# A graph layer with a mixture of low-rank experts on one core: two steps' operations in a new order, the gathers in two runs, the gate's sum on ScalarE

## The chip, the core and the metric

The kernel runs on one core of a Trainium2 chip. Its time is device time in microseconds (us). Of the kernel before there are three runs: 1904.98, 1907.07 and 1908.52 us; their median, 1907.07, is the time that the prediction starts from. The names of the engines in the rows are: PE for TensorE's matmuls, PEld for its weight loads, DVE for VectorE, ACT for ScalarE, POOL for GpSimd, SP for SyncE, which issues most DMAs.

## The reference

There are 128 graphs of 128 nodes, with 1024 features each, in float32. The matrix `adj` holds counts between nodes (about 3% of the entries are set).

```python
x = x + elu(gat(layernorm(x), adj))      # one layer of graph attention
x = x + moe(layernorm(x))                # a mixture of low-rank experts

def gat(h, adj):                         # 16 heads of 64 features
    Wh = (h @ W) split into heads
    e = leaky_relu(Wh . a1 + Wh . a2)    # per node of a row, per head
    att = softmax(where(adj == 0, -9e15, e)) * adj
    return att @ Wh, heads side by side

def moe(y):                              # 8 experts of rank 16, 2 of them chosen
    gates = softmax over the top two of y[row 0 of the graph] @ router_w.T
    return sum_e gates[e] * ((y @ lora_down[e].T) @ lora_up[e].T)
```

The experts of a graph are chosen by its first row alone, and all of its 128 rows then use them.

## The kernel before

**Tiles and steps.** Graphs are taken in pairs (64 pairs, q = 0 to 63) and in groups of four (32 groups, g). Step q multiplies pair q by W, does the attention, the two layer norms and the residual sums of pair q-1, and one half of the experts' work for the group that the pairs before form: odd and even steps together make a group, so everything repeats every two steps. Steps 0 and 1, and those after the last pair, are ordered by another function (`at_the_ends`).

**The product by W** is Strassen's with seven products of half blocks, `M1` to `M7`, each in two halves (`M1a`, `M1b`): eight passes on TensorE for one half (L529), accumulated in a bank of PSUM. Reading a bank is done on VectorE (`u2`, `u4`, `c22`, `c21`, `c12`: L536) or ScalarE (`p1`: L541); `f` adds a part on GpSimd (`add_other`, L553). M3 of two pairs is done jointly by an inner product of seven parts, `I1` to `I7` (L593), which is read by `ip`, `ipa`, `r` and `s` (L599 to L611). The pair sums `ps0` to `ps3` (L462) and inner sums `is0` to `is3` (L472) make the products' inputs on GpSimd. The result's high and low parts come from `hi` (ScalarE, L664) and `lo` (VectorE, L668).

**The attention** of graph t of a pair: `A` (four matmuls, L723), `h` (L729), `x` (L736), `e` (ScalarE, L739), `y` (L746), then the second layer norm's mean on GpSimd (`n`, L751), its squares on ScalarE (`q`, L755) and, on GpSimd, the small `ss` (L776 to L783) and part of the inner product, `ipa` (L602). `t` copies a graph's halves on ScalarE (L796) and transposes them by a DMA; `rj` (L802) and `jn` (L823) put them together again. `st` and `rs` are the first layer norm's statistics and rstd (L401 to L406).

**The experts' work** of a group: `ro`, `sr`, `rp` (L852 to L858) and `L` (a router matmul, L891) give eight logits a graph; `ch0` and `ch1` choose the top two; `ra` takes one exponential on ScalarE (L938); `wg` makes the gates on VectorE (L944 to L946); `fr` computes the rows to fetch (L955, L958); `fe` gathers them by nine indirect DMAs on GpSimd's queue (eight at L968 for the down matrices, one at L972 for the up matrices); `D` is the down matmul (L982, 64 small matmuls), `dn` its gate on ScalarE (L993), `U0` and `U1` the up matmuls for the two halves of the features (L1002, eight instructions in two pairs of banks, one bank for each graph), and `v00`, `v01`, `v10`, `v11` add two graphs' banks each to the residual on VectorE (L1011). `v10` and `v11` also issue the output's stores on SP's queue (L1014). Each double bank has two buffers, which `pd`, `pu`, the attention's `ph` and the inner products share: U1's first pair of banks must have been read by v00, its second by v01.

**Loads.** `lx` loads the next pair (L152), `lt` its transpose x_t (L157), `lc` the counts of three groups ahead (L161), `la` the counts transposed (L166). `ac` (L479 `nz`, L482 `n`) and `an` (L488 to L493) prepare the mask of a group two ahead from the counts.

**What sets the order.** Nothing is reordered by a scheduler. A step from 2 to 63 runs the names of one of two lists, `EVEN` or `ODD`, one after the other, and issues each operation at once. A name with a minus sign belongs to the step before. So the lists alone are the order of every engine's queue and of every DMA queue:

```python
for name in (EVEN, ODD)[q % 2]:
    if q > 2 or not name.endswith("-"):
        do(q, name)
```

Of the kernel before, what the change touches and what calls it, by code (L numbers as in the profile page):

```python
# [8 lines left out]
F32 = mybir.dt.float32  # L9
# [4 lines left out]
AF = mybir.ActivationFunctionType  # L14
ALU = mybir.AluOpType
# [6 lines left out]
TINY = 1e-30  # L22

EVEN = """
lo0- e1- M5b- wg- M5a- M7a- y1- ac- M7b- u4- c22- ps0- ro1- c12- n0- q0- t0- D- M4b- t1-
st0- n1- ps1- dn- st1- q1- an- U0- M1b v00- ss- v01- rj0- M4a- U1- c21- ro0- v10- aw hi3-
hi1- M1a ps3- v11- rs- hi2- lo1- lo3- M6a lc- rj1- jn0- lo2- p1 A0 jn1- lt pe ps2- M6b A1 u2
""".split()

ODD = """  # L30
aw2- M2b- M2a- M5b- h0- hi0- ps0- ps1- x0- sc0- ps3- lx- h1- M5a- lo0- is0- M7a- x1- e0- y0-
e1- u4- is2- ro0- M7b- y1- n0- c22- q0- is1- ro1- sr- is3- st0- n1- I7- I6- t0- ps2- I1- ip-
q1- M4a- ipa- st1- r- ss- I5- rp- I4- s- M4b- c21- rs- L- hi2- I3- ch0- d1- lo2- hi3- I2-
ch1- t1- fr- M6a d0- aw rj0- M1b M1a hi1- la- pe lo1- aw2 lo3- M6b A0 jn0- h0 lx p1 jn1- u2
A1 x0 rj1- fe- h1 M2b x1 lt e0 M2a f hi0 sc0 ra- y0
""".split()


# [2 lines left out]
def adj_ffn_kernel(  # L41
# [16 lines left out]
    nc = tc.nc  # L58
    B, N, D = x.shape
    P = 128  # L60
    KC = D // P
# [5 lines left out]
    R = ER // E  # L67
    TOP = 2
# [5 lines left out]
    NG, _, G, _ = adj.shape  # L74
# [8 lines left out]
    work = ctx.enter_context(tc.tile_pool(name="work", bufs=2))  # L83
# [12 lines left out]
    GRP = {}  # L96
# [831 lines left out]
    def own(val, name):  # L928

        mine = small.tile([P, G * TOP], F32, tag="own", name="own", bufs=2)  # L930
        nc.vector.tensor_tensor(mine, val.rearrange("p g s -> p (g s)"), slot, ALU.mult)
        got = small.tile([P, 1], F32, tag=name, name=name)
        nc.vector.tensor_reduce(got, mine, AX.X, ALU.add)  # L933
        return got

    def ratio(g):
        pr = GRP[g]["pr"]
        nc.scalar.activation(pr[:, 1], pr[:, 0], AF.Exp)  # L938

    def weigh(g):  # L940

        st = GRP[g]
        gate, pr = st["val"][:, 1], st["pr"]
        nc.vector.tensor_scalar(gate[:, :, 0], pr[:, 1], 1.0, None, op0=ALU.add)  # L944
        nc.vector.reciprocal(gate[:, :, 0], gate[:, :, 0])
        nc.vector.tensor_mul(gate[:, :, 1], pr[:, 1], gate[:, :, 0])  # L946
        if g < NG - 1:
            st["gate"] = own(gate, "gate")
# [10 lines left out]
                                op1=ALU.add)  # L959
        st["at"] = at_down, at_up  # L960

    def fetch(g):

        st = GRP[g]
        at_down, at_up = st.pop("at")
        st["down"] = work.tile([P, G * TOP * R, KC], F32, tag="down", name="down", bufs=1)
        for j in range(G * TOP):
            nc.gpsimd.indirect_dma_start(  # L968
                out=st["down"][:, j * R:(j + 1) * R].rearrange("p r k -> p (r k)"), out_offset=None, in_=table,
                in_offset=bass.IndirectOffsetOnAxis(ap=at_down[:, j:j + 1], axis=0))  # L970
        st["up"] = work.tile([P, D], F32, tag="up", name="up", bufs=1)
        nc.gpsimd.indirect_dma_start(  # L972
            out=st["up"], out_offset=None, in_=up_t,
            in_offset=bass.IndirectOffsetOnAxis(ap=at_up[:, 0:1], axis=0))
# [144 lines left out]
    def tasks(q):  # L1119

        g, part = divmod(q - 2, 2)
        i = 2 * q - 2
        more = q + 1 < NQ
        does = pair(q)[0]
        p = q - 1
        does.update({
            "aw": (attention_weights, p), "pe": (exp_weights, p), "aw2": (divide_weights, p),
            "ss": (second_stats, p)})
        for t in range(2):
            y = i + t  # L1130
            does.update({
                f"A{t}": (attend, y), f"h{t}": (weigh_sum, y), f"x{t}": (add_above, y),
                f"e{t}": (exp_sum, y), f"y{t}": (add_below, y), f"n{t}": (less_mean, y),
                f"q{t}": (squares, y), f"t{t}": (turn, y), f"rj{t}": (rejoin, y),
                f"jn{t}": (join, y), f"ro{t}": (first_row, y) if y < B - G else None,
                f"st{t}": (first_stats, 2 * q + 2 + t) if more else None})
        does["rs"] = (first_rstd, q + 1) if more else None
        for n in range(4):
            does[f"ps{n}"] = (pair_sums, q + 1, n) if more else None
        does.update({"lx": (load_x, q + 1) if more else None, "lt": (load_xt, q + 1) if more else None})  # L1140
        if part:
            does.update({
                "wg": (weigh, g), "D": (ffn_down, g), "dn": (gate_down, g),
                "U0": (ffn_up, g, 0), "U1": (ffn_up, g, 1),
                "ac": (group_adj, g + 2) if g + 2 < NG else None,
                "an": (no_entries, g + 2) if g + 2 < NG else None,
                "lc": (load_counts, g + 3) if g + 3 < NG else None})
            for h in range(2):
                for two in range(2):
                    does[f"v{h}{two}"] = (add_up, g, h, two)  # L1150
        else:
            does.update({
                "sr": (spread_rows, g), "rp": (row_parts, g), "L": (logits, g),
                "ch0": (choose, g, 0), "ch1": (choose, g, 1), "fr": (fetch_rows, g),
                "ra": (ratio, g), "fe": (fetch, g),
                "la": (load_adj, q // 2 + 1) if q // 2 + 1 < NG else None})
            for n in range(4):
                does[f"is{n}"] = (inner_sums, q, n)
        return does

    def do(q, name):
# [7 lines left out]
    def between(q):  # L1169

        DOES[q] = tasks(q)
# [3 lines that stand above are left out]
        if q == NQ - 1:  # L1175
            load_all()
            load_router()
            order_all()

    def at_the_ends(q):  # L1180
# [11 lines left out]
        if ffn and not part:  # L1192
            gaps[6] += [(ratio, g), (weigh, g)]
# [120 lines left out]
```

## Time and profile before

| what | number |
|---|---|
| median of three runs | 1907.07 us (1904.98 to 1908.52) |
| profiled execution, its time | 1914.27 us |
| its span | 1912.5 us |
| granted TensorE clock, mean | 0.997 |
| TensorE busy (matmuls) | 1880.3 us, 98% |
| VectorE busy | 1588.2 us, 83% |
| ScalarE busy | 1206.4 us, 63% |
| GpSimd busy | 1005.2 us, 53% |
| DMA over the span | 173 GB/s mean |
| the product by W, all forms (L529) | 958.4 + 487.3 us on PE |
| the gate's sum (L944) | 54.0 us on VectorE in 32 instructions |
| the gathers (L968, L972) | 250.2 + 29.2 us on GpSimd in 279 instructions |
| add_up (L1011) | 170.2 us on VectorE in 248 instructions |
| ffn_up (L1002) | 77.2 us on TensorE in 496 instructions |

How to read it. The profile is one execution, and its busy times are sums of the instructions' durations on an engine. Matmuls are pipelined, so one that has started overlaps the one before; on TensorE the distance between two starts says more than a duration. A row of the timeline has start, duration, engine, line, operation, output and inputs with their shapes, and the count of instructions taken together; a bracket at its end gives the idle time before it and what ended it. A row of the chain has start, duration, engine, the tile and the line. The chain of work that ended last is followed back from the last instruction, at each step to what released it or to the instruction before it on its engine.

### The profile page before, as it was taken

To read this page: it belongs to the slowest core of one execution; us is meant where nothing else is said; L and a number is where in the kernel's file an instruction comes from. 1 tells how busy PE (TensorE), PEld (TensorE's weight loads), DVE (VectorE), ACT (ScalarE), POOL (GpSimd) and SP (SyncE) were. 2 spreads that over 40 slices of the span, in tenths; PEclk is the share of its full clock that TensorE was granted. 3 is DMA by queue.
4 is the path that set the end of the run, shared out by engine and by line. 5 is a ranking of instruction groups with operands and counts; after the bars stand their busy time and mean duration, and the time that the engine had idled before them with its cause. 6 is when DMAs were issued, how large, how long until landed. Compare 5 with 4: busy or idle time off the path is not lost.

```text
span 1912.5 us, 29493 instructions
## 1 busy us (share of the span) xinstructions
PE 1880.3 (98%) x10306; PEld 1530.2 (80%) x10306; DVE 1588.2 (83%) x3356; ACT 1206.4 (63%) x1346; POOL 1005.2 (53%) x1485
## 2 busy tenths in 40 slices
PE   9999999999999999999999999999999999999996
PEld 6887888888887878887888888888888888878883
DVE  6787888888888888887888888888888888888886
ACT  3566666676666666665766666766666666666664
POOL 3546555556545465544565454555455555454640
PEclk9999999999999999999999999999999999999999
DMA  8365555655556655546655556555566556566553
GB/s 318 113 189 137 188 160 178 199 160 166 188 152 186 199 144 174 185 147 191 163 164 188 154 184 199 156 165 188 152 191 199 146 171 187 149 189 200 126 157 108
DMA packets 349100, 330.43 MB, mean 173 GB/s; under 512 B 279196, under 2 KB 281372, under 8 KB 348440
## 3 DMA queue, kind: packets, MB, share of 16 engines
q1 hardware_dynamic: 331224, 286.57, 50.2%
q0 software_dynamic: 17008, 40.91, 7.2%
q8 instruction: 82, 1.34, 0.3%
q10 hardware_dynamic: 720, 1.06, 0.1%
q14 instruction: 66, 0.54, 0.1%
HBM read 194.24 MB, written 68.17 MB: 137 GB/s over the span
## 4 chain that ended last, share of the span: by engine, by line
PE 59%; DVE 23%; ACT 6%; DMA 4%; POOL 3%; issue 3%; SPq 2%; DVEq 0%; POOLq 0%; ACTq 0%
PE pw L529 42%; PE pw L593 7%; PE pu L1002 4%; DVE ph L729 4%; DMA xt<-in_x_t 3%; DVE xn L736 3%; PE ph L723 3%; DVE xn L746 3%; DVE val L944 3%; DVE wh L536 2%; PE ix L593 2%; DVE parts L668 2%; POOL s L462 2%; ACT parts L664 2%; ACT halves L796 1%
## 5 line engine op out<-in xcount | busy, mean ns | idle before, releaser
L529 PE MATMUL pw<-w_sb,xt 128*128 128x260 f32 (+1 forms) x4080 | 958.4, 385 | 9.3 <-DVE parts L668 4.7
L529 PEld LDWEIGHTS pw<-w_sb,xt 128*128 128x128 f32 x4080 | 768.1, 190 | 181.7 <-issue 27.2
L529 PE MATMUL pw<-w_sb,s 128*128 128x260 f32 (+1 forms) x2080 | 487.3, 382 | 0.0
L529 PEld LDWEIGHTS pw<-w_sb,s 128*128 128x128 f32 x2080 | 394.8, 190 | 62.1 <-DVE wh L536 0.9
L968 POOL DMA_INDIRECT down<-table,at_down x248 | 250.2, 1009 | 211.9 <-DVE of_slot L933 135.8
L802 ACT COPY y_t<-tt 128x2048 uint16<-128x2048 uint16 x126 | 313.9, 2491 | 44.6 <-DMA tt<-halves 44.6
L462 POOL TENSOR_TENSOR s<-xt 128x512 f32<-128x512 f32 x64 | 81.4, 1272 | 394.7 <-DMA xt<-in_x_t 370.7
L755 ACT ACTIVATE ph<-xn,acc 128x1024 f32<-128x1024 f32 x128 | 142.8, 1116 | 160.6 <-POOL acc L751 160.6
L796 ACT COPY halves<-xn 128x2048 uint16<-128x2048 uint16 x126 | 235.0, 1887 | 1.3 <-DVE xn L746 1.3
L664 ACT ACTIVATE parts<-wh,rstd 128x512 fp32r<-128x512 f32 x192 | 130.8, 714 | 156.1 <-DVE wh L536 155.8
L1011 DVE SCALAR_TENSOR_TENSOR xn<-pu,rstd,xn 128x512 f32<-128x512 f32 x248 | 170.2, 740 | 17.4 <-PE pu L1002 17.4
L536 DVE TENSOR_TENSOR wh<-pw,wh 128x520 f32<-128x520 f32 (+1 forms) x130 | 90.6, 697 | 103.9 <-PE pw L529 103.8
L729 DVE TENSOR_TENSOR ph<-ph,att 128x1024 f32<-128x1024 f32 x128 | 157.1, 1228 | 20.9 <-PE ph L723 10.2
L723 PE MATMUL ph<-parts,adj_f 128*128 128x512 f32 x512 | 161.7, 437 | 3.2 <-DVE parts L668 1.6
L739 ACT ACTIVATE ph<-ph 128x1024 f32<-128x1024 f32 x128 | 131.1, 1024 | 49.9 <-DVE xn L736 49.4
L746 DVE SCALAR_TENSOR_TENSOR xn<-ph,xn 128x1024 f32<-128x1024 f32 x128 | 155.7, 1216 | 4.9 <-ACT ph L739 4.9
L736 DVE SCALAR_TENSOR_TENSOR xn<-ph,xn 128x1024 f32<-128x1024 f32 x128 | 156.2, 1220 | 2.3
L823 ACT ACTIVATE xn<-xn,off,mul 128x1024 f32<-128x1024 f32 x128 | 158.0, 1236 | 0.0
L401 DVE BATCH_NORM_STATS2 stats<-xn 128x6 f32<-128x512 f32 x248 | 155.6, 670 | 0.0
L668 DVE SCALAR_TENSOR_TENSOR parts<-wh,rstd,parts 128x512 fp32r<-128x512 f32 x192 | 138.8, 751 | 11.0 <-ACT parts L664 10.9
L664 ACT ACTIVATE parts<-pw,rstd 128x512 fp32r<-128x512 f32 x63 | 43.3, 687 | 131.2 <-PE pw L529 131.2
L723 PEld LDWEIGHTS ph<-parts,adj_f 128*128 128x128 f32 x512 | 96.3, 189 | 36.4 <-DVE parts L668 16.3
(201 smaller groups left out, 2206.4 us busy)
## 6 DMA issues: line engine op xcount, KB each, us to landing
xn<-in_x SPq DMA_DIRECT2D x128, 512.0 KB
xt<-in_x_t SPq DMA_DIRECT2D x127, 512.0 KB
out_y<-xn SPq DMA_DIRECT2D x124, 512.0 KB
adj_f<-in_adj_t POOLq DMA_DIRECT2D x32, 256.0 KB
adj_i<-in_adj SPq DMA_DIRECT2D x32, 256.0 KB
down<-table,at_down POOLq DMA_INDIRECT x248
w_sb<-in_w SPq DMA_DIRECT2D x3, 1040.0 KB
wt_sb<-in_w_t SPq DMA_DIRECT2D x1, 2048.0 KB
```

The source lines that it names most:

```text
L529: nc.tensor.matmul(banks[name][:, j, cols], lhs()[:, k, :], w_sb[:, rhs, k, j, cols], start=(fresh and k == 0), stop=(k == KH - 1), skip_g ...
L593: nc.tensor.matmul(bank(name), sums(lhs)[:, k], w_of[rhs][:, k], start=(fresh and k == 0), stop=(k == KI - 1), skip_group_check=not fresh)
L664: nc.scalar.mul(in_two(PARTS[q][:, 0, b]), block, rstd)
L668: nc.vector.scalar_tensor_tensor(in_two(PARTS[q][:, 1, b]), block, rstd, in_two(PARTS[q][:, 0, b].bitcast(F32)), op0=ALU.mult, op1=ALU.sub ...
L723: nc.tensor.matmul(PH[i][:, h], GRP[g]["adj_f"][:, t, :], PARTS[q][:, s, NH * (i % 2) + h], start=(s == 0), stop=(s == 1))
L729: nc.vector.tensor_tensor(ph, ph, ATT[i // 2][:, i % 2, :, None].to_broadcast([P, H, F]), ALU.mult)
L736: nc.vector.scalar_tensor_tensor(X[i], whole(i), 0.0, X[i], op0=ALU.max, op1=ALU.add)
L746: nc.vector.scalar_tensor_tensor(X[i], whole(i), 1.0, X[i], op0=ALU.min, op1=ALU.add, accum_out=acc[:, 0:1])
L796: nc.scalar.copy(halves, X[i].bitcast(U16).rearrange("p (d s) -> p s d", s=2))
L802: nc.scalar.copy(y_of(i).bitcast(U16).rearrange("p k (n s) -> p s k n", s=2), TT.pop(i).rearrange("p (s k) n -> p s k n", s=2))
L968: nc.gpsimd.indirect_dma_start(out=st["down"][:, j * R:(j + 1) * R].rearrange("p r k -> p (r k)"), out_offset=None, in_=table, in_offset=b ...
L1011: nc.vector.scalar_tensor_tensor(y[:, cols], st["pu", h][t], st["rstd"][:, t:t + 1], y[:, cols], op0=ALU.mult, op1=ALU.add)
```

## The change

Both lists are written in a new order. Beside the order, and in it, these things differ:

- The nine gathers get a name each (`fe0` to `fe8`), so that the lists can place them one by one. In the new order seven of them stand together (2, 1, 6, 0, 4, 7, 3; other names between them issue nothing on GpSimd), then come a pair sum (`ps2`) and `rs` on GpSimd, then gather 5 and the gather of the up matrices (8).
- The gate's sum, 1 + the exponential, goes from VectorE (the first instruction of `wg`, L944) to ScalarE, as a second activation of `ra`.
- `ac` goes from the even list to the odd one; `lc`, the counts' load, too. `lt`, the load of the next pair's x_t, comes earlier in both lists.
- On TensorE the even step had D, M4b, U0, M1b, M4a, U1; it now has D, M4b, U0, M4a, U1, M1b, M1a. The attention matmuls of the two graphs in an even step, which stood apart, now stand together behind M6.

Lines behind the exponential move by one to four in the new file: the sum is L941 there, the gathers L971 and L976, ffn_down L986, ffn_up L1006, add_up L1015.

```diff
 EVEN = """
-lo0- e1- M5b- wg- M5a- M7a- y1- ac- M7b- u4- c22- ps0- ro1- c12- n0- q0- t0- D- M4b- t1-
-st0- n1- ps1- dn- st1- q1- an- U0- M1b v00- ss- v01- rj0- M4a- U1- c21- ro0- v10- aw hi3-
-hi1- M1a ps3- v11- rs- hi2- lo1- lo3- M6a lc- rj1- jn0- lo2- p1 A0 jn1- lt pe ps2- M6b A1 u2
+y1- M5b- n1- y0- q1- M7a- u4- wg- f- M7b- n0- an- t0- q0- ro0- D- c22- ps0- ps1- ro1- hi3-
+dn- c12- M4b- U0- ss- M4a- v00- v01- U1- M1b M1a t1- v10- jn0- lo3- hi1- lt rj0- c21- v11-
+lo1- M6a ps2- hi2- ps3- ps0 aw lo2- lx M6b st1- A0 A1 p1 pe rs- rj1- ps1 M2a aw2 M2b hi0 ps3
+u2 h0 x0 sc0 h1 jn1- e0 lo0
 """.split()
 
 ODD = """
-aw2- M2b- M2a- M5b- h0- hi0- ps0- ps1- x0- sc0- ps3- lx- h1- M5a- lo0- is0- M7a- x1- e0- y0-
-e1- u4- is2- ro0- M7b- y1- n0- c22- q0- is1- ro1- sr- is3- st0- n1- I7- I6- t0- ps2- I1- ip-
-q1- M4a- ipa- st1- r- ss- I5- rp- I4- s- M4b- c21- rs- L- hi2- I3- ch0- d1- lo2- hi3- I2-
-ch1- t1- fr- M6a d0- aw rj0- M1b M1a hi1- la- pe lo1- aw2 lo3- M6b A0 jn0- h0 lx p1 jn1- u2
-A1 x0 rj1- fe- h1 M2b x1 lt e0 M2a f hi0 sc0 ra- y0
+M5b- M5a- x1- e1- M7a- M7b- y0- ro0- u4- n0- is0- is2- q0- I1- I7- y1- ip- is1- c22- I6-
+st1- ro1- r- ac sr- is3- n1- M4a- M4b- I2- hi3- la- lx st0- rp- c21- I5- q1- ss- L- t0- ipa-
+I4- ch0- s- lc M6b ch1- lt fr- fe2- t1- fe1- I3- d1- fe6- hi2- fe0- d0- hi1- jn1- fe4- aw
+M6a lo3- pe lo1- jn0- M1b lo2- fe7- aw2 M1a fe3- p1 A1 rj0- ps2- st0 h1 x1 rs- M2a fe5- e1
+A0 M2b u2 M5a ra- sc0 hi0 rj1- h0 x0 e0 fe8- lo0
 """.split()
...
     def ratio(g):
         pr = GRP[g]["pr"]
+        gate = GRP[g]["val"][:, 1]
         nc.scalar.activation(pr[:, 1], pr[:, 0], AF.Exp)
+        nc.scalar.activation(gate[:, :, 0], pr[:, 1], AF.Copy, bias=1.0)
 
     def weigh(g):
 
         st = GRP[g]
         gate, pr = st["val"][:, 1], st["pr"]
-        nc.vector.tensor_scalar(gate[:, :, 0], pr[:, 1], 1.0, None, op0=ALU.add)
         nc.vector.reciprocal(gate[:, :, 0], gate[:, :, 0])
...
-    def fetch(g):
+    def fetch(g, j):
...
-        for j in range(G * TOP):
+        if j < G * TOP:
...
             nc.gpsimd.indirect_dma_start(
                 out=st["down"][:, j * R:(j + 1) * R].rearrange("p r k -> p (r k)"), out_offset=None, in_=table,
                 in_offset=bass.IndirectOffsetOnAxis(ap=at_down[:, j:j + 1], axis=0))
+            return
...
+            for n in range(G * TOP + 1):
+                does[f"fe{n}"] = (fetch, g, n)
```

More of the change, by code (lines that the diff above doesn't have):

```diff
@@ L960, in fetch_rows @@
         st["at"] = at_down, at_up
-    def fetch(g):
+    def fetch(g, j):
         st = GRP[g]
-        at_down, at_up = st.pop("at")
-        st["down"] = work.tile([P, G * TOP * R, KC], F32, tag="down", name="down", bufs=1)
-        for j in range(G * TOP):
+        at_down, at_up = st["at"]
+        if j < G * TOP:
+            if "down" not in st:
+                st["down"] = work.tile([P, G * TOP * R, KC], F32, tag="down", name="down", bufs=1)
             nc.gpsimd.indirect_dma_start(
@@ L1154, in tasks @@
                 "ch0": (choose, g, 0), "ch1": (choose, g, 1), "fr": (fetch_rows, g),
-                "ra": (ratio, g), "fe": (fetch, g),
+                "ra": (ratio, g),
                 "la": (load_adj, q // 2 + 1) if q // 2 + 1 < NG else None})
```

## The prediction

> **What bounds the kernel now.** I read the page first, then the chain that ended last, then the timeline of one group of four graphs, engine by engine. The page and its chain:
>
> ```profile
> PE 1880.3 (98%) x10306; PEld 1530.2 (80%) x10306; DVE 1588.2 (83%) x3356; ACT 1206.4 (63%) x1346; POOL 1005.2 (53%) x1485
> ...
> PE 59%; DVE 23%; ACT 6%; DMA 4%; POOL 3%; issue 3%; SPq 2%; DVEq 0%; POOLq 0%; ACTq 0%
> ```
>
> TensorE has something in flight 98% of the time, so an edit pays only where it takes away a moment in which no new matmul starts. The 23% of VectorE in the chain mean less than they look: that work ran level with TensorE, which was issuing meanwhile. The chain also gives the length of a group. After every ffn_down it lists the same eight matmul passes (M4b), and their starts lie one group apart:
>
> ```profile
> 530.17 2.02 PE pw L529 x8
> ...
> 587.73 2.02 PE pw L529 x8
> ...
> 602.11 6.56 DMA xt<-in_x_t
> ...
> 646.21 2.02 PE pw L529 x8
> ...
> 880.71 1.92 PE pd L982 x64
> 882.63 1.95 PE pw L529 x8
> ```
>
> 587.73 - 530.17 = 57.56 us is the usual group (most are 57.55 to 57.60). 646.21 - 587.73 = 58.48 is a group whose x_t tile landed late. From 184.69 to 1807.13 there are 28 groups in 1622.4 us, 10.5 more than 28 x 57.57: that much the late tiles (and one group of 62.4 us) cost in this execution. It took 1914.27 us for a span of 1912.5, and is 7.2 above the median of the runs, 1907.07. If the usual group is the same in both, the median run holds only some 10.5 - 7.2 = 3.3 us of lateness.
>
> So the question is how many times within a group TensorE's starts hold, before and after. The timeline of TensorE alone, in the group at 1111:
>
> ```profile
> 1115.46 1.33 PE L1002 MATMUL pu<-up,dn 32*128 32x512 f32 x8
> 1116.71 3.77 PE L529 MATMUL pw<-w_sb,xt 128*128 128x260 f32 x16
> 1120.42 1.14 PE L1002 MATMUL pu<-up,dn 32*128 32x512 f32 x8
> 1121.49 2.02 PE L529 MATMUL pw<-w_sb,xt 128*128 128x260 f32 x8
> ...
> 1124.91 1.57 PE L723 MATMUL ph<-parts,adj_f 128*128 128x512 f32 x4
> ```
>
> Differences of starts are what counts. U1 (1120.42) lets the next product start 1.07 later; U0 (1115.46) needs 1.25, because its second pair of banks came free late.
>
> **Part 1: the gate's sum.** 31 of the 32 sums lie in the groups. The three rows that price one:
>
> ```profile
> 1164.05 1.30 POOL L553 TENSOR_TENSOR other<-other,wh 128x520 f32<-128x520 f32 x1
> 1164.67 1.93 DVE L944 TENSOR_SCALAR val<-pr 128x4 f32<-128x4 f32 x1
> 1165.30 1.26 POOL L462 TENSOR_TENSOR s<-xt 128x512 f32<-128x512 f32 x1
> ```
>
> Four elements take 1.93 us, and 0.16 where GpSimd is idle (the line's minimum). The sum ends when GpSimd's second operation ends, at 1166.6. VectorE so loses 1.93 - 0.16 = 1.77 us a group, and the chain runs through it. But TensorE was issuing all that time; the first product that feels it is M4b, which waits for the read of its banks (L536, c12). After ffn_down a group normally takes 1113.51 - 1111.38 = 2.13 us to the next product; in the group of 880.71, whose sum did not wait, 1.92. So of 1.77 us TensorE sees 0.21. On ScalarE the sum is one small activation: 0.16 to 0.22 us by L550 and L938, 32 x 0.2 = 6 us on an engine that is 63% busy. It stands ahead of the first high half (hi0), whose product has more room than that; I take 0, and at most 0.2 a group (6 us) without that cover.
>
> **Part 2: what the new order takes away on TensorE.** Per group:
> - M4b behind ffn_down: 0.21, as above.
> - U0: 1.25 - 1.07 = 0.18. It waited for ScalarE's squares (L755); in the new order both squares are issued before ffn_down's successor, well ahead.
> - The first graph of an even step: its four matmuls at 1124.91 let the next product start at 1126.31, 1.40 later; the second, 1127.88 to 1129.00, needs 1.12. The 0.28 between is the wait for the low half (L668), which the eight add_up operations pushed back. In the new order both graphs of the even step stand together behind M6, a whole product later: gone.
> - The inner products: the four passes at 1143.90 take 0.95 instead of 0.88 (1139.52 to 1140.40), behind a VectorE read. 0.07, gone, since M4 now stands between.
> Sum 0.74 us, times 30 groups: **-22.2 us**. Lower bound, if half of it returns elsewhere: -11.
>
> **Part 3: what it adds on TensorE.** The old list has U0, M1b, M4a, U1; the new one has U0, M4a, U1. Each half product is eight passes. U1 writes the banks that v00 and v01 must have read, and these are two add_up operations each:
>
> ```profile
> 1116.80 2.67 DVE L1011 SCALAR_TENSOR_TENSOR xn<-pu,rstd,xn 128x512 f32<-128x512 f32 x4
> ...
> 1121.59 1.41 DVE L1011 SCALAR_TENSOR_TENSOR xn<-pu,rstd,xn 128x512 f32<-128x512 f32 x2 [0.37 <-PE pu L1002]
> ```
>
> The second row shows how soon add_up can begin: 1121.59 - 1120.42 = 1.17 after the start of its U, with VectorE waiting. Four of them take 2.67. So the second pair of banks is free at 1.17 + 2.67 = 3.84 after U0's start, 3.90 with the 0.06 that a matmul needs after its release. TensorE is there sooner: 1.07 for U0, then M4a's eight passes 1.86 (1121.49 to the next product at 1123.35), and 0.09 more for entering U: 3.02. It waits 3.90 - 3.02 = 0.88, and the row of U0 shows that a late second pair delays the next product in full. Before, with M1b between as well, U1 came 1.0 us after the last of the four had ended (1116.80 + 2.67 = 1119.47, U1 at 1120.42): no wait. Price 0.86 to 0.88, times 30: **+26 us**. Bounds: 0.34 if the second pass of the first pair (0.53 later) fills part of the hole (+10); 1.1 if VectorE is not yet free when U0 is done (+33). I take the middle, since VectorE then has nothing else queued ahead.
>
> Parts 2 and 3 together: 26 - 22.2 = +3.8, or 0.12 a group: the usual group would be 57.57 + 0.12 = 57.7 us.
>
> **Part 4: transfers.** SP's order changes. Before, the even step's x_t loads stood behind four output stores and the counts (1122.37 to 1128.5), and GpSimd waited for them: 370.7 us in 30 waits at L462. The inner sums and their products follow at once, so a late tile is a late group. Now the loads stand between the second and third store, the counts go to the odd step, and the odd step's x_t is asked for before its transposes instead of near the step's end. That is 2 to 3 us earlier, more than the 0.5 to 0.9 by which usual late tiles were late. -3.3 of the median run (bounds 0 and -3.3), and half of the 2.6 us by which the group at the start (124.52 to 184.69) is too long: -1.3. Nine gathers at 1.25 us apart are 11 us of GpSimd in both; in two runs, the third pair sum (1.27) goes between, which feeds M7, a product later. I take 0; without cover the last two end 2.2 us later (1.27 and the 0.93 of first_rstd), still ahead of ffn_down. A waiting gather holds GpSimd's pair sums behind it, as before.
>
> **Sum.** On the profiled execution: 1914.27 + 26 - 22.2 - 10.5 - 1.3 = 1906.3. On the median: 1907.07 + 26 - 22.2 - 3.3 - 1.3 = 1906.3. I say 1906. A measurement of this kernel can tell about 0.2%, 3.8 us, from no change; this is within it.
>
> **A rule weighed.** nz (L479, 0.42 us) moves from a place where GpSimd pauses to one beside GpSimd's train of small operations (L776 to L783, then L602), some 2 us long. In the trace the sum at L944 was held across two GpSimd operations that followed each other at once, while nz itself, at the start of the kernel beside pair sums, took at most 1.01. The Trainium skill, "SBUF — State Buffer", section "SBUF: two separate sides", says that the pair of ports which VectorE and GpSimd share is an exclusive lock, held for one whole instruction by whichever comes first. By that rule nz would wait for one operation, at most the 0.72 of L777, and the sum would stay at 1906; by the row of L944 it may wait for the train.
>
> **Rivals.**
> - Slower, nz held: VectorE has 0.65 (r) + 1.11 (ac) + 1.3 (st0) + 1.1 (rp) = 4.2 us to do between the end of the inner product I6 and the router's matmul, and TensorE 5.26 (M4, I2, I5). Some 0.7 us remain after the latencies. Held like L944, nz takes 1.93 instead of 0.42, 1.51 more: 0.8 us a group, +24: 1930. It decides from a hold of 0.7 us on. For: L944's row. Against: nz's own longest, 1.01, and that most of these small operations depend on each other, which leaves gaps.
> - Faster, U1's hole half filled: +10 instead of +26: 1890. Against: U0's row.
> - The order does not bring the tiles earlier, or its other products wait a tenth each: within the forecast, 1908 to 1916.
>
> **Chances.** Forecast (prices cancel) 0.60; nz or a like hold 0.25; hole filled 0.15. The forecast's own range is 1896 to 1916, ten to each side: half of part 2 coming back is +11, and the upper bound of part 3 is +7; downward I take the same, since the hole may be filled in part. Spread evenly it splits 0.22 below 1903.3, 0.23 within 0.2%, 0.15 above 1910.9. Faster 0.22 + 0.15 = 0.37, same 0.23, slower 0.15 + 0.25 = 0.40. The range runs from near the faster case (1890) to near the slower one (1930): 1892 to 1926, which leaves out half of each rival, 0.2 in all.
>
> **What would show it.** Right: groups of about 57.7; L1002's second call with TensorE idle near 0.9 us behind L1011, 30 times; no wait of L529 for L536 behind ffn_down; few groups over 58. Wrong: U1 without a wait, nz over 1 us with the router's matmul waiting, or L462 still waiting for x_t with inner products behind it.

## The result, and the profile after

In 20 runs each, taken side by side, the changed kernel took 1909.96 us (1909.54 to 1910.93) and the kernel before 1906.42 (1904.98 to 1908.78): a ratio of 1.0018 with a 95% interval of 1.0011 to 1.0025. It is 3.5 us slower, where 1 us faster had been forecast; the time lies inside the range of 1892 to 1926. The profiled execution took 1910.64 us for a span of 1908.9, 3.6 less than the profiled execution before, which was a late one.

The page of the changed kernel, busy times and chain:

```profile
PE 1888.8 (99%) x10306; PEld 1538.5 (81%) x10306; DVE 1534.5 (80%) x3324; ACT 1228.7 (64%) x1378; POOL 1014.2 (53%) x1485
...
PE 96%; DVE 2%; ACT 1%; POOL 1%; issue 0%; DVEq 0%; ACTq 0%; POOLq 0%
```

VectorE's 23% of the chain has become 2%, and VectorE is 53.7 us less busy, about the 54.0 us of the gate's sum. So the chain shows hardly a wait of TensorE's any more. Yet TensorE is busy for 8.5 us more. Where these are, its timeline shows, in the group at 1198:

```profile
1220.27 1.99 PE L986 MATMUL pd<-y_t,down 128*32 128x128 f32 x64
1222.19 2.02 PE L530 MATMUL pw<-w_sb,xt 128*128 128x260 f32 x8
1224.14 1.14 PE L1006 MATMUL pu<-up,dn 32*128 32x512 f32 x8
1225.21 2.02 PE L530 MATMUL pw<-w_sb,xt 128*128 128x260 f32 x8
1227.16 2.06 PE L1006 MATMUL pu<-up,dn 32*128 32x512 f32 x8
1229.15 3.77 PE L530 MATMUL pw<-w_sb,xt 128*128 128x260 f32 x16
```

From ffn_down to the next product it is 1.92 us now (2.13 before), from U0 to the next 1.07 (1.25 before), but from U1 to the next 1.99, where it was 1.07. That is the hole that was forecast. VectorE shows the other side of it:

```profile
1225.31 2.73 DVE L1015 SCALAR_TENSOR_TENSOR xn<-pu,rstd,xn 128x512 f32<-128x512 f32 x4 [3.01 <-PE pu L1006]
1228.34 1.41 DVE L1015 SCALAR_TENSOR_TENSOR xn<-pu,rstd,xn 128x512 f32<-128x512 f32 x2 [0.30 <-PE pu L1006]
```

The four add_up operations begin 1.17 us after U0 starts and end at 1228.04. About 0.04 later the second four of U1's matmuls start, and 1.07 behind that the next product. The wait of 0.92 us counts as busy in the page, because the records of U1's first four matmuls run on until the second four have started.

All 30 groups, from one router matmul to the next, are now 57.80 to 57.82 us long; before, the usual one was 57.57 and the others reached 62.24. So the usual group got 0.24 longer, and none is late any more.

### The profile page after: what moved, and what is told of

It reads as the page before. It is cut to its first block, busy times and chain, and to the rows that moved or that the text cites. A ratio compares the mean times of both kernels' runs of the same rounds, so it can differ in the third digit from the quotient of the medians.

```text
span 1908.9 us, 29370 instructions
## 1 busy us (share of the span) xinstructions
PE 1888.8 (99%) x10306; PEld 1538.5 (81%) x10306; DVE 1534.5 (80%) x3324; ACT 1228.7 (64%) x1378; POOL 1014.2 (53%) x1485
## 4 chain that ended last, share of the span: by engine, by line
PE 96%; DVE 2%; ACT 1%; POOL 1%; issue 0%; DVEq 0%; ACTq 0%; POOLq 0%
PE pw L530 70%; PE pw L594 7%; PE ph L724 6%; PE pu L1006 5%; PE pd L986 3%; PE ix L594 3%; POOL down L971 0%; PE pu L1071 0%; PE idle L216 0%; ACT y_t L803 0%; PE pl L892 0%; ACT ph L740 0%; PE rows L294 0%; DVE xn L737 0%; DVE ph L730 0%
## 5 line engine op out<-in xcount | busy, mean ns | idle before, releaser
L530 PE MATMUL pw<-w_sb,s 128*128 128x260 f32 (+1 forms) x2080 | 482.3, 382 | 0.0
L971 POOL DMA_INDIRECT down<-table,at_down x248 | 257.9, 1040 | 243.7 <-DVE of_slot L934 174.9
L797 ACT COPY halves<-xn 128x2048 uint16<-128x2048 uint16 x126 | 238.9, 1896 | 65.5 <-DVE n L483 44.6
L1015 DVE SCALAR_TENSOR_TENSOR xn<-pu,rstd,xn 128x512 f32<-128x512 f32 x248 | 171.6, 744 | 105.4 <-PE pu L1006 105.4
L463 POOL TENSOR_TENSOR s<-xt 128x512 f32<-128x512 f32 x64 | 82.2, 1284 | 321.5 <-DMA xt<-in_x_t 277.3
L665 ACT ACTIVATE parts<-wh,rstd 128x512 fp32r<-128x512 f32 x192 | 137.4, 717 | 129.9 <-DVE wh L615 110.5
L724 PE MATMUL ph<-parts,adj_f 128*128 128x512 f32 x512 | 154.7, 434 | 2.9 <-DVE parts L669 2.3
L756 ACT ACTIVATE ph<-xn,acc 128x1024 f32<-128x1024 f32 x128 | 142.3, 1112 | 22.7 <-POOL acc L752 22.7
L665 ACT ACTIVATE parts<-pw,rstd 128x512 fp32r<-128x512 f32 x63 | 43.3, 687 | 158.1 <-PE pw L530 115.5
L669 DVE SCALAR_TENSOR_TENSOR parts<-wh,rstd,parts 128x512 fp32r<-128x512 f32 x192 | 138.4, 748 | 2.3 <-ACT parts L665 2.3
L542 ACT COPY wh<-pw 128x520 f32<-128x520 f32 (+1 forms) x64 | 38.0, 593 | 125.9 <-DVE parts L669 86.8
L752 POOL TENSOR_SCALAR acc<-acc 128x1 f32<-128x1 f32 x128 | 29.9, 234 | 164.8 <-DVE xn L747 164.8
```

Source lines behind the costliest of these rows:

```text
L530: nc.tensor.matmul(banks[name][:, j, cols], lhs()[:, k, :], w_sb[:, rhs, k, j, cols], start=(fresh and k == 0), stop=(k == KH - 1), skip_g ...
L665: nc.scalar.mul(in_two(PARTS[q][:, 0, b]), block, rstd)
L724: nc.tensor.matmul(PH[i][:, h], GRP[g]["adj_f"][:, t, :], PARTS[q][:, s, NH * (i % 2) + h], start=(s == 0), stop=(s == 1))
L797: nc.scalar.copy(halves, X[i].bitcast(U16).rearrange("p (d s) -> p s d", s=2))
L971: nc.gpsimd.indirect_dma_start(out=st["down"][:, j * R:(j + 1) * R].rearrange("p r k -> p (r k)"), out_offset=None, in_=table, in_offset=b ...
L1015: nc.vector.scalar_tensor_tensor(y[:, cols], st["pu", h][t], st["rstd"][:, t:t + 1], y[:, cols], op0=ALU.mult, op1=ALU.add)
```

## The experiments

Each was compared with runs of the kernel before taken on the same chip in turn. That kernel's median differed from one such set of runs to the next: 1906.42 in the result's, then 1906.57, 1906.91, 1910.42 and 1911.15 us on four different chips. The unchanged new kernel, run again beside the last of these, shows what that means. Times are to be compared within a set first.

**The new kernel again** (no edit).

> The new kernel unchanged, beside the kernel before in the same rounds, as the measure for the other edits of this kernel. Theory A (its groups are 57.81 us in every run, and the kernel before carries a load of late x_t tiles that differs from run to run): 1910 with a scatter under 1.5 us, whatever the kernel before takes there; the ratio to it moves with the kernel before alone, 0.999 to 1.002. Theory B (the new order itself is 0.2% slower everywhere): the ratio is 1.0018 again.

1910.38 us (1909.72 to 1911.34), beside 1911.15 of the kernel before: a ratio of 0.9998 (0.9989 to 1.0007). That is theory A: the new kernel stays where it was, with 29 of 30 groups of 57.79 to 57.82 us in its profile, and the kernel before moves. That its late tiles are what moves it is likely and not shown, since no profile of it was kept in these sets. The nearest is that of the kernel before with the sum alone moved (below), taken in the set of 1910.42: its 30 groups are 12.6 us longer than 30 x 57.57. So whether the change costs 0.2% or nothing depends on the set of runs.

**M1b between M4a and U1 again,** and c21, the read of M4a's bank, from behind M1a to just behind U1.

```diff
-... U0- ss- M4a- v00- v01- U1- M1b M1a t1- v10- jn0- lo3- hi1- lt rj0- c21- v11-
+... U0- ss- M4a- v00- v01- M1b U1- c21- M1a t1- v10- jn0- lo3- hi1- lt rj0- v11-
```

> The new order with two moves in the even step: M1b goes between M4a and U1 again, and c21 (the read of M4a's bank) from behind M1a to just behind U1. Theory A (the group is 0.24 us longer because U1 starts one half product too soon after U0 and waits for v01): the 0.92 us wait of U1 goes, since 1.86 us of passes now stand in front of it, nothing else comes, and the group is 57.81 - 0.92 = 56.89 us; 30 groups give -28, about 1882 us. Theory B (VectorE or a bank is the bound there, and the hole only moves): another wait of about 0.9 us shows on M1a, M6a or the attention's matmuls, and the time stays at 1910. Theory C (the earlier M1b uses its x_t tile sooner and meets late tiles): groups of 57 to 59 us of uneven length, 1885 to 1905.

1886.45 us (1884.55 to 1886.82), beside 1910.42 before: 0.9875 (0.986 to 0.989). TensorE's timeline in this kernel:

```profile
1210.81 3.77 PE L530 MATMUL pw<-w_sb,xt 128*128 128x260 f32 x16
1214.52 1.14 PE L1006 MATMUL pu<-up,dn 32*128 32x512 f32 x8
1215.59 2.02 PE L530 MATMUL pw<-w_sb,xt 128*128 128x260 f32 x8
```

Sixteen passes now lie ahead of U1, and it takes 1.07 us. The shortest groups are 56.87 us, 0.94 less; that is theory A. But they are uneven, 57.03 on average and 58.03 at the most. So C has a small share, and the total is 24 us less than the new kernel's, not 28. The two moves were not tried one by one.

**The other way round: the kernel before, with M1b moved behind U1.**

```diff
-... U0- M1b v00- ss- v01- rj0- M4a- U1- c21- ro0- v10- aw hi3- hi1- M1a
+... U0- v00- ss- v01- rj0- M4a- U1- M1b c21- ro0- v10- aw hi3- hi1- M1a
```

> The kernel before with nothing changed but the place of M1b, which goes from between U0 and M4a to behind U1, as in the new order. Theory A (the hole in front of U1 is made by this move alone): U1 waits 0.7 to 0.9 us for v01 in every group, +21 to +27 us: 1930 to 1937. Theory B (the hole needs the rest of the new order, with the squares and the weighing elsewhere): less than 0.3 us a group, under 1920.

1922.01 us (1920.98 to 1922.30), beside 1911.15: 1.0057 (1.0041 to 1.0072).

```profile
1238.15 1.99 PE L1002 MATMUL pu<-up,dn 32*128 32x512 f32 x8
1240.08 2.24 PE L529 MATMUL pw<-w_sb,xt 128*128 128x260 f32 x9
```

U1 takes 1.93 instead of 1.07: the hole is there by this move alone, at 0.86 us. The groups grew by less, from 57.57 to 58.15: the first attention of the step, which had waited 0.28 for its low half, now comes later and no longer waits. Two of the 30 groups are late (59.90 and 60.49), 0.15 us or more above the usual, where in the profile of the kernel before it is 13; perhaps a longer group leaves the tiles more time. So the mechanism was A's; the total was half of what A gave, since a hole of 0.86 takes over a wait that came behind it and, it seems, some of the lateness.

**Only the place of the x_t loads, in the kernel before.**

```diff
-hi1- M1a ps3- v11- rs- hi2- lo1- lo3- M6a lc- rj1- jn0- lo2- p1 A0 jn1- lt pe ps2- M6b A1 u2
+hi1- lt M1a ps3- v11- rs- hi2- lo1- lo3- M6a lc- rj1- jn0- lo2- p1 A0 jn1- pe ps2- M6b A1 u2
...
-ch1- t1- fr- M6a d0- aw rj0- M1b M1a hi1- la- pe lo1- aw2 lo3- M6b A0 jn0- h0 lx p1 jn1- u2
-A1 x0 rj1- fe- h1 M2b x1 lt e0 M2a f hi0 sc0 ra- y0
+ch1- lt t1- fr- M6a d0- aw rj0- M1b M1a hi1- la- pe lo1- aw2 lo3- M6b A0 jn0- h0 lx p1 jn1- u2
+A1 x0 rj1- fe- h1 M2b x1 e0 M2a f hi0 sc0 ra- y0
```

> The kernel before with nothing changed but the place of the x_t loads: in the even step between hi1 and M1a (so between the second and third output store), in the odd step behind ch1. Theory A (the order of SP's queue makes the late tiles): no group over 57.7 us is left, and the time falls by the 5 us that separate the median before (1906.4) from 30 usual groups: 1901, with runs that scatter by less than 1.5 us. Theory B (the DMA engines' load makes them late, wherever the loads stand): the same time as before, 1906, and the same scatter of 4 us.

1904.00 us (1903.32 to 1906.66), beside 1910.42: 0.9971 (0.996 to 0.9982). 26 of 30 groups are 57.53 to 57.63 us, one 59.62, three 57.8 to 57.9. The place of the loads in SP's queue by itself takes away 6.4 us, measured against the kernel before on the same chip. That is theory A, but not all of it: the time is not its 1901, four groups are still over 57.7, and the runs scatter by 3.3 us, not by less than 1.5.

**The reverse: the new kernel with the loads where they were.**

```diff
-... hi1- lt rj0- c21- v11- lo1- M6a ps2- hi2- ps3- ps0 aw ...
+... hi1- rj0- c21- v11- lo1- M6a ps2- hi2- ps3- lt ps0 aw ...
...
-I4- ch0- s- lc M6b ch1- lt fr- fe2- ... rj1- h0 x0 e0 fe8- lo0
+I4- ch0- s- lc M6b ch1- fr- fe2- ... rj1- h0 x0 lt e0 fe8- lo0
```

> The new order with the x_t loads where the kernel before had them: in the even step behind all four output stores, in the odd step at its end. Theory A (the early loads are what keeps the new kernel's groups even): groups over 58 us come back, as in the kernel before, and the time is 3 to 10 us longer than 1910.4, with a scatter of several us. Theory B (the new order of the products gives room enough, or U1's wait of 0.92 us takes the lateness up): 1910 with groups of 57.81 us.

1911.19 us (1909.77 to 1912.29), beside 1906.91: 1.0020 (1.0011 to 1.0030). That is about 1 us more than the new kernel in its own sets of runs. 27 of 30 groups are 57.80 to 57.82 us, and one of the others reaches 58.82. Nearer to B. GpSimd's pair sums wait as long for tiles as in the kernel before; the group row:

```profile
L463 POOL TENSOR_TENSOR s<-xt 128x512 f32<-128x512 f32 x64 | 82.0, 1282 | 376.1 <-DMA xt<-in_x_t 373.7
```

373.7 us of waits, 370.7 before and 277.3 in the new kernel, and TensorE hardly notices. In the kernel before, the inner sums, which the inner products need, start 0.08 us behind the last pair sum; here they mostly start 1.8 us behind it or more, so a late tile has some room. In the kernel before the earlier loads were enough to remove most of the lateness; in the new order they are hardly needed.

**Only the gate's sum, in the kernel before.** ScalarE's second activation comes in, VectorE's sum goes, and the lists stay.

> The kernel before with nothing changed but the gate's sum, which goes to ScalarE as in the new kernel. Theory A (the 0.21 us wait of M4b behind ffn_down comes from the sum that GpSimd holds): the wait goes, -0.2 x 30 = -6 us, 1900. Theory B (another instruction on VectorE is held by the same GpSimd operations in its place, or TensorE only arrives earlier at U0's second pair of banks): no change within 2 us, with 0.2 us more in U0's wait.

1909.77 us (1908.02 to 1913.10), beside 1910.42: 1.0000 (0.9991 to 1.0009). Theory B. GpSimd's timeline at the place:

```profile
1163.70 1.30 POOL L553 TENSOR_TENSOR other<-other,wh 128x520 f32<-128x520 f32 x1
1164.95 1.27 POOL L462 TENSOR_TENSOR s<-xt 128x512 f32<-128x512 f32 x1
```

And VectorE's:

```profile
1164.33 0.17 DVE L945 RECIPROCAL val<-val 128x4 f32<-128x4 f32 x1
1164.53 1.72 DVE L946 TENSOR_TENSOR val<-pr,val 128x4 f32<-128x4 f32 x1
1166.29 0.17 DVE L931 TENSOR_TENSOR own<-val,slot 128x8 f32<-128x8 f32 x1
```

The next multiplication, four elements with two inputs from SBUF, is held in the sum's place, 1.72 us, up to the end of GpSimd's second operation. The reciprocal, with one input, passes beside the first. M4b's wait behind ffn_down goes all the same (1.92 in nearly all groups), but it comes back at U0, one product on, whose way to the next product grows from 1.25 to 1.46 us. U0 there waits for the squares on ScalarE, as before, and TensorE only reaches it earlier.

**Only the gate's sum, in the new kernel:** back on VectorE as the first instruction of wg, and the lists stay.

> The new kernel with nothing changed but the gate's sum, which goes back to VectorE as the first instruction of the gate's weighing (wg). Theory A (the place in the order, not the engine, decides: what is short here is U1's wait): the sum takes 0.16 to 1.9 us, and TensorE sees at most 0.2 us of it behind ffn_down: 1910 to 1916. Theory B (on VectorE the sum is held beside the pair and inner sums of GpSimd whatever the order, and in the new order the reads c22 and c12 that free the banks stand close behind it): the group grows by 1 us or more, 1940 or more.

1910.42 us (1909.88 to 1911.04), beside 1910.42: 1.0002 (0.9993 to 1.0011). It is the new kernel's time. Theory A, at its lower end. The group row of the sum:

```profile
L946 DVE TENSOR_SCALAR val<-pr 128x4 f32<-128x4 f32 x32 | 5.1, 160 | 0.3 <-ACT pr L940 0.3
```

0.16 us on VectorE too. In the new order the weighing runs at 1220.9, where GpSimd does only operations of 0.2 to 0.3 us (L489 to L494), not between two long ones. The order removed the hold; in it, the move to ScalarE did nothing.

**The nine gathers in one run, in the new kernel.**

```diff
-... M1a fe3- p1 A1 rj0- ps2- st0 h1 x1 rs- M2a fe5- e1 ...  x0 e0 fe8- lo0
+... M1a fe3- p1 A1 rj0- fe5- fe8- ps2- st0 h1 x1 rs- M2a e1 ...  x0 e0 lo0
```

> The new order with the nine gathers in one run: gather 5 and the gather of the up matrices go ahead of the third pair sum, where the other seven are. Theory A (the split costs and gains nothing): the third pair sum starts two gathers, 2.5 us, later; it ended 3.2 us before the first product that reads its tile, so 0.7 us are left and the group stays 57.81: 1910. Theory B (the pair sum then also falls beside VectorE's low halves, is held, and is late): that product waits 0.5 to 2 us a group, 1925 to 1970.

1980.10 us (1979.39 to 1980.44), 1.0361 (1.0345 to 1.0377) beside 1911.15. The size is beyond B's, and the reason is another. Groups are 60.06 us on average, 2.25 longer. The chain of this kernel in one group, from the last gather on, without its rows of "issue" (0.02 to 0.09 us each):

```profile
1196.35 0.94 POOL up L976
1197.31 1.28 POOL xt L463
1198.67 0.23 POOL rstd L406
1198.97 0.74 POOL rstd L407
1199.74 0.70 ACT parts L665
1200.46 0.76 DVE parts L669
1201.27 3.77 PE pw L530 x16
```

What hangs behind the gathers is the rstd of the first layer norm (L406, L407). hi0 (L665) and lo0 (L669) need it; they read the bank in PSUM that M7 writes, and M7 must wait until that is done; TensorE's timeline gives 1.75 us of idle time ahead of it, ended by lo0. The next run tests that.

**All nine in one run, but rs ahead of them;** against the run before:

```diff
-... lc M6b ch1- lt fr- fe2- ...  st0 h1 x1 rs- M2a e1
+... lc M6b ch1- lt rs- fr- fe2- ...  st0 h1 x1 M2a e1
```

> The new order with all nine gathers in one run, as in the run before that cost 70 us, but with the first layer norm's rstd (rs, two small GpSimd operations) ahead of the first gather; the third pair sum stays behind the nine. Theory A (what the nine in a run held back was the rstd, which the high and low halves hi0 and lo0 wait for, and these free the bank that M7 writes): that wait goes, the group is 57.8 to 58.0 us again, 1910 to 1916. Theory B (the late third pair sum, which M7 reads, holds as well): M7 still waits 1 to 2 us a group, 1940 to 1970.

1909.05 us (1908.58 to 1910.34), beside 1906.91: 1.0012 (1.0002 to 1.0021). All groups are 57.80 to 57.82 us. Theory A: it was the rstd, and the third pair sum, still behind nine gathers, holds nothing in the groups. The split into seven and two is one of two ways to get the rstd out in time; by itself it is worth nothing.

**The end of the kernel.** In the two profiles the new kernel takes 2.8 us longer than the one before from its 31st router matmul, the last that closes a group, to the end (74.2 instead of 71.4; 73.6 when it was run again). From its chain there, GpSimd and then ScalarE:

```profile
1849.70 0.74 POOL rstd L407
...
1850.46 0.69 ACT parts L665
...
1853.55 0.91 ACT ph L740
1854.46 1.99 ACT w_sb L1037
1856.44 1.15 ACT ph L756 x2
```

A copy of the down matrices (L1037) lies ahead of the squares (L756), which free the bank for ffn_down. In the next run the copy went behind the last hi2:

> The new kernel with one move, at its end alone: the large ScalarE copy of the down matrices (L1037, 2.06 us) goes from the end of the last odd step to behind the last hi2. Theory A (ffn_down's one wait of 1.54 us near the end comes from that copy, which runs ahead of the squares whose bank it needs): the wait goes, 1910.4 - 1.5 to 2 = 1908.5 us. Theory B (the copy is waited for later anyway): 1910.4.

1910.89 us (1910.10 to 1912.32), beside 1906.57: 1.0022 (1.0013 to 1.0031). It gave nothing. ffn_down's wait is gone, but the copy now stands in the chain 13 us later, before another copy that the last transposes wait for:

```profile
1867.82 1.99 ACT w_sb L1037
1869.81 2.37 ACT y_t L803
```

B, then: its 2 us were moved on ScalarE, not taken away; the end is still 74.1 us. The kernel before has the same copy ahead of its last squares (L1033, 2.07 us), so the copy alone could not have been the difference.

The head of the chain points elsewhere, to the rstd behind the gathers, which the high half (L665) waits for. The run with rs ahead of the gathers bears on it. Its ffn_down at the end waits 0.27 us, where the new kernel's waits 1.37; the two rows, the new kernel first:

```profile
1857.63 2.29 PE L986 MATMUL pd<-y_t,down 128*32 128x128 f32 x64 [1.37 <-ACT ph L756]
...
1856.89 2.29 PE L986 MATMUL pd<-y_t,down 128*32 128x128 f32 x64 [0.27 <-ACT ph L756]
```

Its end takes 72.1 us, and between 1846 and 1866 neither a gather nor the rstd is in its chain. So 1.5 to 2.1 us of the 2.2 to 2.8 probably hang on the rstd. It is one profile, and that run differs by the run of gathers too; what the rest comes from stays open.

**The fastest order.** M1b and c21 as above; the even step's x_t load from behind hi1 to just behind c21, ahead of the output stores; and that same copy moved.

```diff
-... M4a- v00- v01- U1- M1b M1a t1- v10- jn0- lo3- hi1- lt rj0- c21- v11-
+... M4a- v00- v01- M1b U1- c21- lt M1a t1- v10- jn0- lo3- hi1- rj0- v11-
...
             load_router()
-            order_all()
...
                 if name.endswith("-"):
                     do(q, name)
+                if name == "hi2-":
+                    order_all()
```

> The new order with three moves: M1b between M4a and U1 and c21 behind U1, as in the run before; the x_t load in the even step from behind hi1 to just behind c21, ahead of the output stores; and at the end of the kernel the large ScalarE copy of the down matrices (L1037, 2.06 us) from the end of the last odd step to behind the last hi2. Theory A (what was left in the run with M1b moved are late tiles, 0.09 us a group, and ffn_down's 1.54 us wait near the end comes from that copy ahead of the squares): all groups 56.88 us, and the end 1.5 to 2.8 us shorter: 1886.4 - 30 x 0.09 - 2 = 1881 to 1883 us. Theory B (the earlier transfer collides with the transposes, or the copy delays the high halves at the end instead): 1885 to 1888.

1881.93 us (1881.78 to 1883.34), beside 1911.15: 0.985 (0.9837 to 0.9864). 24 of 30 groups are 56.87 to 56.91 us. The load's place took 3.5 us off the groups against the profile of the run with M1b alone; the end is 0.4 shorter, not the 2 that A counted on.

**The same without the change's two named parts:** the sum on VectorE, and the nine gathers in one run with rs ahead.

> The fastest order so far (M1b, c21, x_t load and end copy moved, 1881.9 us) with the two named parts of the change taken back: the gate's sum on VectorE, and the nine gathers in one run, with rs ahead of them. Theory A (neither the engine of the sum nor the split of the gathers is worth anything by itself; only where rs and the weighing stand counts): 1881.9 again, groups of 56.88 us. Theory B (they give room that the shorter group needs): 1884 or more.

1883.07 us (1882.44 to 1884.63), beside 1906.57: 0.9877 (0.9862 to 0.9892). The shortest groups are the same, 56.87; 13 of 30 are over 56.93 (6 in the run before). That is 1.1 us more, and in another set of runs, so between A and a small B it stays undecided. It looks like 1 us at the most that hangs on the two parts.

## Why the prediction was wrong

**Right: the group, term by term.** M4b behind ffn_down 0.21 (2.13 to 1.92), U0 0.18 (1.25 to 1.07), the first attention 0.28 (1.40 to 1.12) and the inner products 0.07 all went; U1's hole was 0.92 where 0.88 was said; the four add_up operations take 2.73 us and not 2.67. Two rivals fell with it. The hole is not half filled. And nz isn't held:

```profile
L480 DVE TENSOR_SCALAR nz<-adj_i 128x512 f32<-128x512 int32 x32 | 14.3, 447 | 1.0 <-DMA adj_i<-in_adj 1.0
```

0.447 us on average, as before (0.454). But that was close, and partly luck. In all 30 groups nz starts in the pause between two dependent GpSimd operations, about 0.05 us ahead of the second one (L778), and it is that one which gets longer, 0.95 to 0.96 us where it takes 0.71 to 0.73 elsewhere:

```profile
1194.37 0.42 DVE L480 TENSOR_SCALAR nz<-adj_i 128x512 f32<-128x512 int32 x1
...
1194.41 0.96 POOL L778 TENSOR_TENSOR rstd<-rstd,half_pow 128x2 f32<-128x2 f32 x1
```

What nz would have taken behind L778, no run shows.

**Wrong: the sum's sign, by four small terms.** The forecast was 8.0 us below the profiled execution before; measured were 3.6. Of these 4.4 us:
- U1's hole: 0.92 x 30 = 27.6 where 26 stood, +1.6.
- A wait that part 3 didn't see: in the odd step the two attentions, which stood together, now stand apart with M2a between them. M2a's first weight load waits for its bank, which p1's copy (L542) reads, and M2a's first pass lasts 0.28 us to the next where 0.22 is usual: 30 x 0.066 = +2.0. So the group became 57.81 where 57.69 was forecast.
- The end: +2.8. The prediction has no term for the work after the last group; there the new lists leave the rstd behind the gathers, and ScalarE waits for it.
- Lateness and the start gave more than was counted: in the profiled groups 30 x 57.57 = 1727.1, and they took 1740.2: 13.1 us too long, all gone, where 10.5 + 1.3 had been put in. The time up to the first router matmul fell by 0.6, which is within its scatter (100.3 to 101.0 in the profiles of either kernel and its variants). Together -1.9.

That makes +4.5, which is the 4.4 but for rounding. The row of M2a's weight load, after the group's first attention at 1207.54:

```profile
1208.62 1.61 PEld L530 LDWEIGHTS pw<-w_sb,xt 128*128 128x128 f32 x8 [0.24 <-ACT wh L542]
```

**The step that failed** is the sum itself, which takes everything outside its terms for unchanged. The work after the last group stood at nothing without a reason, and it took 2.8 us more (2.2 when the new kernel was run again). Part 2 asked only after the even step's attentions and part 3 only after U1, so M2a's wait in the odd step was not in it: +2.0. U1's hole was put 1.6 too low. These 6.4 us turned a forecast gain of 0.8 on the median into a loss.

Part 4's "-3.3 of the median run" was wrong too, but the other way. It set one profiled execution against a median of three and took the difference for the lateness. As an estimate from the profile: with all lateness gone the kernel before would be at 1914.27 - 13.1 = 1901.2, so the 20-run median of 1906.42 holds 5.2, and the medians of the other sets of runs up to 10. That the change took 5.2 away and not 3.3 hid 1.9 of the 6.4. The change takes 5.2 away and adds 7.2 (the groups), 2.8 (the end) and -0.6 (the start): 1906.42 - 5.2 + 9.4 = 1910.6, against 1909.96 measured. That the loads' place removes lateness in the kernel before is shown by the run with the loads alone; that this lateness is no fixed number was not considered.

**Part 1 gave the gain to the wrong cause.** It put M4b's 0.21 us down to the sum's move to ScalarE. In the old order that move does free M4b, but the next multiplication is held in the sum's place, U0 takes the wait over, and nothing is gained; in the new order the sum could have stayed on VectorE. **Part 4's price of 0 for the two runs of gathers** was right in the groups by luck: it looked at the gathers and at the third pair sum, and not at first_rstd, named in the same sentence only for its length. In this order the rstd is the piece that hangs behind them, at 70 us when all nine stand ahead of it, and probably at some 2 us at the end of the kernel as it is.

## What to carry to other kernels

When a list of operations fixes all queues, a change of order is priced by the distances between TensorE's starts, wait by wait; that gave the group to 0.12 us in 57.6. The prologue, the end and whatever scatters from run to run need terms of their own, since in a kernel this tight they decide the sign. And an order that looks spent may hide one hole that a single move closes: M1b before U1 (with c21 moved) was worth 24 us, where the rewrite without it was worth nothing. The rewrite had made that hole itself, and the hole had eaten its 0.74 us a group.

## What the runs showed of the hardware

A short VectorE operation can wait for two GpSimd operations. At 1164.53, in the run with the sum alone moved, the multiplication of four elements was ready while GpSimd ran an operation up to 1165.0; GpSimd then started its next one, and VectorE came in only when that ended, 1.72 us in all instead of 0.16. The Trainium skill, "SBUF — State Buffer", section "SBUF: two separate sides", says that the pair of ports goes to whichever operation starts first, for one whole instruction. By that, the wait would be the 0.5 us that were left of the first operation; the rows show two GpSimd operations, one behind the other, ahead of VectorE. In the kernel before it is no accident of one group: 27 of the 32 sums (1.87 to 1.95 us) start during the first of two such operations and end with the second. Two with a single operation beside them end with that one (0.68 and 0.72), and three with none beside them take 0.16 to 0.17.

The kernel before differs between sets of runs by more than the change moves, by the estimate above with 5 to 10 us of late tiles. In the new kernel's two profiles only one group of 60 is over 57.82, at 57.91, and its medians in its two sets of runs were 1909.96 and 1910.38.
